# A second graph layer that reads stored transposed 0/1 rows instead of the adjacency matrix

## The chip, the cores and the metric

The kernel runs on one core of a Trainium2 chip. A core has four compute engines that each run their own instruction stream in order: PE (TensorE, matrix products; its weight loads are listed apart as PEld), DVE (VectorE), ACT (ScalarE) and POOL (GpSimd). SP (SyncE) issues most of the DMA transfers, POOL the indirect ones. Engines wait for each other through semaphores. The metric is the device time of one execution in microseconds (us), lower is better.

## What is computed

There are 16 batches of a graph with 1024 nodes and 64 features. `adj` is a symmetric 0/1 matrix with ones on its diagonal. Layer 0 removes some neighbours of every node ("dilation"), takes weighted quantiles of the features of those left, and runs a two-layer MLP. Layer 1 sums the features over the full adjacency and runs a second MLP. Both end in a residual and a layer norm.

```python
nb = (adj_ > 0) & (~eye)[None]                # neighbours without the node itself
m = nb.sum(-1)
rank = jnp.cumsum(nb, axis=-1) - 1
skip = jnp.where(m > 10, (m + 1) // 2, 1)
removed = nb & do_dil[..., None] & ((rank + 1) % skip[..., None] == 0)
rem = removed | jnp.swapaxes(removed, 1, 2)
...
# layer 0: agg = 0.25 q(0.25) + 0.5 q(0.5) + 0.25 q(0.75) over the neighbours left
x = _layernorm(x + (relu((x + agg) @ W1 + b1) @ W2 + b2) * mask)
# layer 1, on the full adjacency
messages = jnp.einsum('bij,bjh->bih', adjacency, h)
dh = jnp.tanh(jnp.concatenate([h, messages], -1) @ W1 + b1) @ W2 + b2
x = _layernorm(x + dh)
```

The edge updates of the second layer's reference don't reach its output and are not computed.

## The kernel before

A tile is 128 nodes, so a batch has eight tiles. The batches are taken in groups of 2, 4, 4, 4 and 2. Three kinds of work run for different groups at once.

**Lists** (`list_batch`, for the group that comes next). SP loads `adj` tile by tile into `a` (128x1024 f32, three buffers, L622) and `x` into the end of the row `nb` (L625). DVE clears the diagonal block (L623) and writes `nb` as 0/1 in bf16 (L626). ACT copies `nb` into `r`, only for the row sums that its accumulator gives (L630). PE transposes `nb` (L652), ACT copies that to `nb_t` (L654, two buffers), PE counts ranks with it in `p_rank` (L658, L660), ACT and DVE turn them into the removed edges (L662, L664). PE subtracts both directions of the removed edges in `p_val` (L672 to L675), ACT writes what is left back to `nb` (L677), and POOL scatters the rows to DRAM in order of degree (`order`, L712).

**Chunks** (`Chunk`, `ChunkByPE`, for the current group). `fetch_lists` loads rows of `order` (`row`, two buffers, L806), `fill` finds the neighbours in it and gathers their features, 1012 times on POOL (L846); the PE kind instead loads `row_p` (two buffers, L957), transposes it and selects by products with 0/1 matrices (`p_slots`, L990). `select` sorts with a network of minima and maxima on DVE (L875), forms the quantiles, runs the first MLP through the PSUM tiles `p_g`, `p_h` and `p_y` (L899 to L908; `p_y` has the single buffer of the tag "y"), and scatters the result to `x1` in DRAM (L916).

**Second layer** (`messages`, for the group before). Per batch, `x1` is loaded (L1018). Then, for each of the eight block rows (`QT` is 1), a row of `adj` is loaded again into `a` (L1024), PE transposes its eight blocks in f32 (`p_adj`, L1029), ACT copies them to `adj_t` (L1030), PE transposes `x1` (`p_x`, L1035) and sums the messages in f32 (`p_msg`, L1039), ACT copies both to `node_t` (L1036, L1041), and `p_z`, tanh and `p_d` follow (L1043 to L1048). DVE adds the bias to each block row (L1049). After the last one DVE adds `x1` (L1051), the layer norm runs, and SP stores the batch (L1053).

The loop at the end of the function (L1097 on) gives out steps of these generators in proportion to an estimate of each chunk's work (`Side`). A scheduler of the framework then orders the instructions of each engine; what the generators' order gives are priorities, not the final order. DMAs from SP and ACT share eight completion semaphores in turn, and a transfer waits until the one that last used its semaphore is complete. Pools give a tile's next user the buffer when the last reader is done. When the last group's chunks are over, the messages of its two batches run alone. `amiss` and `halves` hold tests of the data; if one fails, a general version of the whole computation follows (L1258), which does not run here.

Of the kernel before, what the change touches and what calls it, by code (L numbers as in the profile page):

```python
# [416 lines left out]
def kernel(  # L417
# [23 lines left out]
    QT = 1  # L441
# [13 lines left out]
    off_diag = const.tile([P, P], BF16, name="off_diag")  # L455
    nc.vector.tensor_scalar(off_diag, ident, -1.0, 1.0, op0=ALU.mult, op1=ALU.add)
# [4 lines left out]
    off_diag_f = const.tile([P, P], F32, name="off_diag_f")  # L461
    nc.vector.tensor_copy(off_diag_f, off_diag)
# [22 lines left out]
    zero = const.tile([P, BINS], F32, name="zero")  # L485
    nc.vector.memset(zero, 0.0)
# [30 lines left out]
    for i, (at, _, _) in enumerate(NETS[KTOP]["places"]):  # L517
        nc.gpsimd.memset(place_top[:, :, i], float(at))
    amiss = const.tile([P, B * NT], F32, name="amiss")
# [82 lines left out]
    class Group:  # L602
# [3 lines left out]
        def __init__(self, b0, count):  # L606
            self.b0, self.count, self.tiles, self.run = b0, count, count * NT, P // count
            self.order = [hbm.tile([N, ROW // 2], I32, name=f"order{b0 + i}") for i in range(count)]
            self.x1 = hbm.tile([count * N, C], F32, name=f"x1_{b0}")
            self.parts = []  # L610

    def list_batch(g, b):

        nbs, gone = [], []
        for half_b in range(2):
            at = slice(b * NT + half_b * HT, b * NT + (half_b + 1) * HT)

            m = rows.tile([P, 2, HT], F32, name="m")
            for t in range(half_b * HT, (half_b + 1) * HT):
                blk = slice(t * P, (t + 1) * P)  # L620
                a = rows.tile([P, N], F32, name="a", bufs=3)
                nc.sync.dma_start(a, adj[b, blk, :])  # L622
                nc.vector.tensor_mul(a[:, blk], a[:, blk], off_diag_f)  # L623
                nb = held.tile([P, ROW], BF16, name="nb")
                nc.sync.dma_start(nb[:, XCOL:].bitcast(F32), x[b, blk, :])  # L625
                nc.vector.tensor_scalar(nb[:, :N], a, 0.0, None, op0=ALU.is_gt)  # L626
# [12 lines left out]
            mh = halves[:, at]  # L639
            nc.vector.tensor_add(mh, m[:, 0], m[:, 1])  # L640
            nc.vector.tensor_scalar(mh, mh, 0.5, 0.25, op0=ALU.mult, op1=ALU.add)
            nc.vector.tensor_scalar(skip, mh, ROUND, -ROUND, op0=ALU.add, op1=ALU.add)
            nc.vector.scalar_tensor_tensor(do, mh, 0.5 * T_THRESH + 0.25, mask[:, at],
                                           op0=ALU.is_gt, op1=ALU.mult)
            nc.vector.scalar_tensor_tensor(want, skip, 1.0, do, op0=ALU.add, op1=ALU.mult)
            nc.vector.tensor_scalar(biases[0], skip, -3.0, -2.0 * FAR, op0=ALU.mult, op1=ALU.add)
            nc.vector.scalar_tensor_tensor(biases[1], m[:, 0], 2.0, biases[0], op0=ALU.mult, op1=ALU.add)
            for t in range(half_b * HT, (half_b + 1) * HT):
                nb, r, col = nbs[t], gone[t], slice(t - half_b * HT, t - half_b * HT + 1)
                p = ps_t.tile([P, N], BF16, name="p_nb", tag="tr")  # L650
                for j in range(NT):
                    nc.tensor.transpose(p[:, j * P:(j + 1) * P], nb[:, j * P:(j + 1) * P], ident_h)  # L652
                nb_t = rows.tile([P, N], BF16, name="nb_t")
                nc.scalar.copy(nb_t, p)  # L654

                for h in range(2):
                    p = ps_m.tile([P, HALF], F32, name="p_rank", tag="rv", bufs=3)
                    nc.tensor.matmul(p, far_h, nb[:, h * HALF:(h + 1) * HALF], start=True, stop=False)  # L658
                    for c in range(HT):
                        nc.tensor.matmul(p[:, c * P:], nb_t[:, (h * HT + c) * P:(h * HT + c + 1) * P],  # L660
                                         reach[:, :HALF - c * P], start=False, stop=c == HT - 1)
# [25 lines left out]
        nc.vector.tensor_scalar(low, deg, float(BINS - 1), None, op0=ALU.min)  # L687
# [8 lines left out]
        nc.vector.tensor_tensor_scan(base[:, 1:], zero, p[:, :BINS], 0.0, op0=ALU.add, op1=ALU.add)  # L696
# [89 lines left out]
    class Chunk:  # L786
# [12 lines left out]
        def fetch_lists(self):  # L799
# [3 lines left out]
            for t in range(self.t0, self.t0 + self.n):  # L803
                row = nets.tile([P, N], BF16, name="row")
# [57 lines left out]
        def select(self):  # L862
# [19 lines left out]
            for h in range(0, n, HT):  # L882
# [23 lines left out]
                p_y = ps_m.tile([P, HT, C], F32, name="p_y", tag="y", bufs=1)  # L906
# [15 lines left out]
    class ChunkByPE(Chunk):  # L922
# [13 lines left out]
        def fill(self):  # L936
# [8 lines left out]
            for q in range(g.count // 2):  # L945
# [9 lines left out]
                for i in range(2):  # L955
                    row = nets.tile([P, N], BF16, name="row_p")
# [57 lines left out]
    def messages(g, b):  # L1014

        x1 = work.tile([P, NT, C], F32, name="x1_n", bufs=1)
        n0 = (b - g.b0) * N
        nc.sync.dma_start(x1, g.x1[n0:n0 + N, :].rearrange("(t p) c -> p t c", p=P))  # L1018
        d = work.tile([P, NT, C], F32, name="d", bufs=1)
        for h in range(NT // QT):  # L1020
            adj_t = nets.tile([P, NT, QUART], F32, name="adj_t", bufs=1)
            for t in range(QT):
                a = rows.tile([P, N], F32, name="a", bufs=3)
                nc.sync.dma_start(a, adj[b, (h * QT + t) * P:(h * QT + t + 1) * P, :])  # L1024
                for q in range(2):
                    p = ps_t.tile([P, HT, P], F32, name="p_adj", tag="ta")
                    for j in range(HT):
                        col = (q * HT + j) * P
                        nc.tensor.transpose(p[:, j, :], a[:, col:col + P], ident)  # L1029
                    nc.scalar.copy(adj_t[:, q * HT:(q + 1) * HT, t * P:(t + 1) * P], p)  # L1030
                yield
# [6 lines left out]
            for j in range(NT):  # L1038
                nc.tensor.matmul(p[C:2 * C, :QUART], x1[:, j, :], adj_t[:, j, :],  # L1039
                                 start=(j == 0), stop=(j == NT - 1))  # L1040
# [5 lines left out]
            p_d = ps_m.tile([P, QT, C], F32, name="p_d", tag="y", bufs=1)  # L1046
            for t in range(QT):
                nc.tensor.matmul(p_d[:, t, :], z_t[:, t * P:(t + 1) * P], w2b_s, start=True, stop=True)  # L1048
            nc.vector.tensor_add(d[:, h * QT:(h + 1) * QT], p_d, b2b_r[:, None, :].to_broadcast([P, QT, C]))  # L1049
            yield  # L1050
        nc.vector.tensor_add(d, d, x1)  # L1051
# [45 lines left out]
    for s in range(-LEAD, len(plan)):  # L1097
# [48 lines left out]
    nc.vector.tensor_tensor(amiss, amiss, halves, op=ALU.max)  # L1146
    nc.vector.tensor_reduce(worst, amiss, AX.X, ALU.max)
# [14 lines left out]
    nc.vector.memset(ones_row, 1.0)  # L1162
    ps_t = ctx.enter_context(tc.tile_pool(name="ps_t_g", bufs=2, space=PSUM))
# [7 lines left out]
    def dilate(adj_b, mask_b):  # L1171
# [3 lines left out]
        for t in range(NT):  # L1175
            blk = slice(t * P, (t + 1) * P)
            a = rows.tile([P, N], F32, name="a")
# [173 lines left out]
```

## Time and profile before

| | us |
|---|---|
| median of three timed runs (3123.43 to 3137.13) | 3128.27 |
| span of the profiled execution | 3776.8 |
| PE busy in it | 2604.1 |
| DVE busy | 2394.6 |
| ACT busy | 1582.8 |
| POOL busy | 1522.6 |

The profiled execution is a fifth longer than the timed ones. A line of a group reads: line of the source, engine, operation, what is written and read, shapes and count, then busy time, mean ns of one, and the time that the engine stood idle just before these instructions with what ended most of it. A line of a wait reads: who waited, for whom, us in total, times, longest us. "issue" means that the trace shows nothing that was waited for. PEclk is the share of PE's full clock that was granted, 0.815 on average over this span.

### The profile page before, as it was taken

What the parts mean: (1) busy time and instruction counts of PE and PEld (TensorE: products, weight loads), DVE (VectorE), ACT (ScalarE), POOL (GpSimd) and SP (SyncE); (2) the same over time, 40 slices, a digit from 0 to 9 for tenths busy, and PEclk for the clock granted to TensorE, in tenths of its full rate; (3) what the DMA queues carried; (4) which work ended last, traced back from release to release, by engine and by line L of the source; (5) the groups of instructions that cost most, each with busy time, mean ns of one, the idle gap of its engine ahead of it and who ended that gap; (6) DMA issues with size and microseconds to landing.
All of it is one profiled execution on the core that took longest, in us unless ns stands there. A gap on an engine that the chain in (4) does not pass through costs nothing. (4 is left out here: it accounts for less than half of the span.)

```text
span 3776.8 us, 65923 instructions
## 1 busy us (share of the span) xinstructions
PE 2604.1 (69%) x25076; PEld 1957.5 (52%) x25076; DVE 2394.6 (63%) x5580; ACT 1582.8 (42%) x4045; POOL 1522.6 (40%) x1512
## 2 busy tenths in 40 slices
PE   5545767484875777756887598747879366677777
PEld 2424544262654555535765376525657255565565
DVE  4546774483867766846886467737879368675461
ACT  6523546452433435533554255413445133343353
POOL 3253262436335423652462524462552554423310
PEclk8866888696987887867988798768989677788898
DMA  3401133141312222131333122212222121121222
GB/s 122 132 20 57 52 88 122 46 117 32 95 44 76 80 69 65 43 102 43 93 95 98 41 82 75 68 35 72 78 75 54 39 76 55 39 68 47 61 68 77
DMA packets 221333, 264.34 MB, mean 70 GB/s; under 512 B 147443, under 2 KB 148050, under 8 KB 221008
## 3 DMA queue, kind: packets, MB, share of 16 engines
q1 hardware_dynamic: 174288, 189.31, 17.1%
q0 software_dynamic: 46720, 70.74, 7.0%
q8 instruction: 199, 3.26, 0.4%
q14 instruction: 126, 1.03, 0.1%
HBM read 218.20 MB, written 46.40 MB: 70 GB/s over the span
## 5 line engine op out<-in xcount | busy, mean ns | idle before, releaser
L846 POOL DMA_INDIRECT slots_a<-in_x_dram,idx x1012 | 1185.5, 1171 | 940.0 <-issue 290.2
L990 PE MATMUL p_slots<-hot,parts 128*64 128x256 bf16 (+1 forms) x12288 | 807.7, 275 | 296.6 <-issue 239.5
L990 PEld LDWEIGHTS <-parts 128*64 128x64 bf16 x12288 | 653.2, 115 | 444.3 <-issue 402.1
L982 DVE TENSOR_SCALAR hot<-val 128x2048 bf16<-128x2048 bf16 x456 | 307.3, 693 | 323.0 <-remote 279.9
L916 POOL DMA_INDIRECT x<-y,ids x128 | 165.7, 1295 | 826.4 <-DVE y L558 633.1
L875 DVE TENSOR_TENSOR slots_b<-slots_a 128x256 f32<-128x256 f32 (+14 forms) x582 | 356.4, 627 | 151.2 <-remote 58.6
L1001 ACT COPY slots_a<-p_slots 128x512 f32<-128x512 f32 (+2 forms) x136 | 73.3, 539 | 765.9 <-PE p_slots L990 326.1
L899 PE MATMUL p_g<-ident,terms 128*64 128x128 f32 x1988 | 299.0, 306 | 77.4 <-ACT terms L897 63.2
L1039 PE MATMUL p_msg<-adj_t,x_n 128*64 128x128 f32 x2048 | 288.4, 292 | 65.2 <-issue 53.6
L899 PEld LDWEIGHTS p_g<-ident,terms 128*64 128x64 f32 x1988 | 254.7, 155 | 118.0 <-ACT terms L897 89.8
L1039 PEld LDWEIGHTS p_msg<-adj_t,x_n 128*64 128x64 f32 x2048 | 241.2, 146 | 98.0 <-issue 73.8
L875 DVE TENSOR_TENSOR slots_a<-slots_b 128x256 f32<-128x256 f32 (+11 forms) x526 | 286.2, 556 | 0.6
L660 PE MATMUL p_rank<-reach,nb_t 128*128 128x512 bf16 (+3 forms) x1024 | 204.2, 337 | 90.0 <-ACT nb_t L654 59.6
L662 ACT ACTIVATE gone<-p_rank,s 128x512 bf16<-128x512 f32 x256 | 168.0, 685 | 123.5 <-PE p_rank L660 54.8
L1029 PE MATMUL p_adj<-ident,a 128*128 128x128 f32 x1024 | 191.3, 302 | 39.2 <-ACT adj_t L1030 13.4
L660 PEld LDWEIGHTS <-nb_t 128*128 128x128 bf16 x1024 | 99.8, 108 | 228.3 <-issue 89.0
L1049 DVE TENSOR_TENSOR d<-p_d,b2b_r 128x64 f32<-128x64 f32 x128 | 28.2, 221 | 285.0 <-PE p_d L1048 167.6
L825 DVE MAX8 key<-code 128x8 f16<-128x1024 f16 x170 | 207.4, 1220 | 2.0 <-DVE code L827 0.5
L630 ACT ACTIVATE gone<-nb 128x512 bf16<-128x512 bf16 x256 | 159.8, 627 | 114.2 <-DVE nb L626 96.0
L712 POOL DMA_INDIRECT order<-nb,at_i x128 | 147.7, 1154 | 147.8 <-DVE at_i L708 58.9
L875 DVE TENSOR_TENSOR slots_b<-slots_b 128x256 f32<-128x256 f32 (+11 forms) x310 | 197.7, 638 | 0.4
L677 ACT ACTIVATE nb<-p_val 128x512 bf16<-128x512 f32 x256 | 151.6, 596 | 90.0 <-remote 53.6
(189 smaller groups left out, 4682.3 us busy)
## 6 DMA issues: line engine op xcount, KB each, us to landing
a<-in_adj_dram SPq DMA_DIRECT2D x256, 512.0 KB
row_p<-order SPq DMA_DIRECT2D x64, 256.0 KB
slots_a<-in_x_dram,idx POOLq DMA_INDIRECT x1012
row<-order SPq DMA_DIRECT2D x192, 64.0 KB
nb<-in_x_dram SPq DMA_DIRECT2D x128, 32.0 KB
row<-order SPq DMA_DIRECT2D x32, 128.0 KB
x_s<-in_x_dram SPq DMA_DIRECT2D x16, 256.0 KB
x_n<-x SPq DMA_DIRECT2D x16, 256.0 KB
```

Source lines behind the costliest of these rows:

```text
L630: nc.scalar.activation(r[:, cols], nb[:, cols], AF.Copy, accum_out=m[:, h, t - half_b * HT:t - half_b * HT + 1])
L660: nc.tensor.matmul(p[:, c * P:], nb_t[:, (h * HT + c) * P:(h * HT + c + 1) * P], reach[:, :HALF - c * P], start=False, stop=c == HT - 1)
L662: nc.scalar.activation(r[:, h * HALF:(h + 1) * HALF], p, AF.Abs, bias=biases[h][:, col], scale=2.0)
L825: nc.vector.max(key[:, t, r:r + 8], code)
L846: nc.gpsimd.indirect_dma_start(out=self.a[:, at[k], t, :], out_offset=None, in_=x_rows, in_offset=bass.IndirectOffsetOnAxis(ap=idx[:, t, k ...
L875: nc.vector.tensor_tensor(view(rb, ra, [(d[0], d[1 + side]) for d in dims]), view(ab, aa, [(d[0], d[1]) for d in dims]), view(bb, ba, [(d[ ...
L899: nc.tensor.matmul(p[:C, col], terms[:, i], ident, start=False, stop=t == e - 1 and first + i == places - 1)
L916: nc.gpsimd.indirect_dma_start(out=g.x1, out_offset=bass.IndirectOffsetOnAxis(ap=g.local[:, self.t0 + t:self.t0 + t + 1], axis=0), in_=y[: ...
L982: nc.vector.tensor_scalar(hot[:, :, :, e], val, float(inside[at]), None, op0=ALU.is_equal)
L990: nc.tensor.matmul(p[i * C:(i + 1) * C, o:o + w], g.parts[2 * q + i][:, c, h], hot[:, c, i, :w], start=c == 0 and h == 0, stop=c == NT - 1 ...
L1029: nc.tensor.transpose(p[:, j, :], a[:, col:col + P], ident)
L1039: nc.tensor.matmul(p[C:2 * C, :QUART], x1[:, j, :], adj_t[:, j, :], start=(j == 0), stop=(j == NT - 1))
```

## The change

- List stage: DVE no longer clears the diagonal or makes `nb`. ACT copies `a` into `nb` in bf16, with the row sums from its accumulator, so `nb` now has the diagonal; 1 is subtracted from the half that holds it, and one more matmul each in `p_rank` and `p_val` takes it out. Beside it DVE compares `a` with itself and with zero and counts (`plain`), a test that all of `adj` is 0 or 1. The diagonal is loaded apart, one transfer of 1024 single elements per batch (`own_edge`), and tested at the end.
- `nb_t` is stored to DRAM by a DMA that ACT issues (`turned`, 256 KB per tile).
- Second layer: `QT` is 2, so there are four steps per batch. Each loads two stored tiles (`nbr_t`, one buffer, 512 KB); the transposes and copies of `adj` are gone. `x1` is split once per batch into three bf16 parts, and `p_msg` is 24 bf16 matmuls of 256 columns. `p_d` collects the whole batch in PSUM and is added once.
- Buffers: `row` and `row_p` have one instead of two; `p_y` moves from the tag "y" to the two buffers of "m", and `p_d` holds "y".
- Smaller: `low` is clipped and rounded, a scan's constant operand is `ones_h`, and some constants go or move.

```diff
-    QT = 1
+    QT = 2
...
+            self.turned = [hbm.tile([N, N], BF16, name=f"turned{b0 + i}") for i in range(count)]
...
+        nc.sync.dma_start(own_edge[:, b * NT:(b + 1) * NT], bass.AP(
+            tensor=adj.tensor, offset=adj[b].offset, ap=[[N + 1, P], [P * (N + 1), NT], [1, 1]]))
...
-                nc.vector.tensor_mul(a[:, blk], a[:, blk], off_diag_f)
...
-                nc.vector.tensor_scalar(nb[:, :N], a, 0.0, None, op0=ALU.is_gt)
...
-                    nc.scalar.activation(r[:, cols], nb[:, cols], AF.Copy,
+                    nc.scalar.activation(nb[:, cols], a[:, cols], AF.Copy,
                                          accum_out=m[:, h, t - half_b * HT:t - half_b * HT + 1])
+                nc.vector.scalar_tensor_tensor(r, a, 0.0, a, op0=ALU.is_gt, op1=ALU.is_equal,
+                                               accum_out=plain[:, b * NT + t:b * NT + t + 1])
...
+            nc.vector.tensor_scalar(m[:, half_b], m[:, half_b], -1.0, None, op0=ALU.add)
...
                 nc.scalar.copy(nb_t, p)
+                nc.scalar.dma_start(g.turned[b - g.b0][t * P:(t + 1) * P, :], nb_t)
...
+                    if h == half_b:
+                        c = t - half_b * HT
+                        nc.tensor.matmul(p[:, c * P:], minus_h, reach[:, :HALF - c * P],
+                                         start=False, stop=True)
...
+                if h == t // HT:
+                    nc.tensor.matmul(p[:, (t % HT) * P:(t % HT + 1) * P], minus_h, ident_h,
+                                     start=False, stop=False)
...
-                row = nets.tile([P, N], BF16, name="row")
+                row = nets.tile([P, N], BF16, name="row", bufs=1)
...
-                p_y = ps_m.tile([P, HT, C], F32, name="p_y", tag="y", bufs=1)
+                p_y = ps_m.tile([P, HT, C], F32, name="p_y", tag="m")
...
-                    row = nets.tile([P, N], BF16, name="row_p")
+                    row = nets.tile([P, N], BF16, name="row_p", bufs=1)
...
+        parts = nets.tile([P, NT, 3, C], BF16, name="parts_1", bufs=1)
+        rest = work.tile([P, NT, C], F32, name="x1_rest", tag="wide", bufs=1)
+        for i in range(3):
+            nc.scalar.copy(parts[:, :, i], x1 if i == 0 else rest)
+            if i < 2:
+                nc.vector.tensor_sub(rest, x1 if i == 0 else rest, parts[:, :, i])
         d = work.tile([P, NT, C], F32, name="d", bufs=1)
+        nc.vector.tensor_add(d, x1, b2b_r[:, None, :].to_broadcast([P, NT, C]))
+        p_d = ps_m.tile([P, NT, C], F32, name="p_d", tag="y", bufs=1)
+        yield
         for h in range(NT // QT):
-            adj_t = nets.tile([P, NT, QUART], F32, name="adj_t", bufs=1)
-            for t in range(QT):
-                a = rows.tile([P, N], F32, name="a", bufs=3)
-                nc.sync.dma_start(a, adj[b, (h * QT + t) * P:(h * QT + t + 1) * P, :])
...
-                        nc.tensor.transpose(p[:, j, :], a[:, col:col + P], ident)
-                    nc.scalar.copy(adj_t[:, q * HT:(q + 1) * HT, t * P:(t + 1) * P], p)
-                yield
+            nbr_t = nets.tile([P, QT, N], BF16, name="nbr_t", bufs=1)
+            nc.sync.dma_start(nbr_t, g.turned[b - g.b0][h * QUART:(h + 1) * QUART, :].rearrange(
+                "(t p) n -> p t n", p=P))
...
-                nc.tensor.matmul(p[C:2 * C, :QUART], x1[:, j, :], adj_t[:, j, :],
-                                 start=(j == 0), stop=(j == NT - 1))
+                for i in range(3):
+                    nc.tensor.matmul(p[C:2 * C, :QUART], parts[:, j, i], nbr_t[:, :, j * P:(j + 1) * P],
+                                     start=j == 0 and i == 0, stop=j == NT - 1 and i == 2)
...
-            nc.vector.tensor_add(d[:, h * QT:(h + 1) * QT], p_d, b2b_r[:, None, :].to_broadcast([P, QT, C]))
...
-        nc.vector.tensor_add(d, d, x1)
+        nc.vector.tensor_add(d, d, p_d)
...
-                going = Side(finish_group(groups[i - 1]), groups[i - 1].count * (NT + NT // QT + 1))
+                going = Side(finish_group(groups[i - 1]), groups[i - 1].count * (NT // QT + 2))
```

More of the change, by code (lines that the diff above doesn't have):

```diff
@@ L454 @@
     nc.vector.tensor_copy(ident_h, ident)
-    off_diag = const.tile([P, P], BF16, name="off_diag")
-    nc.vector.tensor_scalar(off_diag, ident, -1.0, 1.0, op0=ALU.mult, op1=ALU.add)
     upper = const.tile([P, P], F32, name="upper")
@@ L460 @@
                             pattern=[[1, P]], channel_multiplier=-1)
-    off_diag_f = const.tile([P, P], F32, name="off_diag_f")
-    nc.vector.tensor_copy(off_diag_f, off_diag)
     minus_h = const.tile([P, P], BF16, name="minus_h")
@@ L484 @@
     nc.vector.memset(eps, EPS)
-    zero = const.tile([P, BINS], F32, name="zero")
-    nc.vector.memset(zero, 0.0)
     number = const.tile([P, B * NT], F32, name="number")
@@ L518 @@
         nc.gpsimd.memset(place_top[:, :, i], float(at))
+    plain = const.tile([P, B * NT], F32, name="plain")
+    own_edge = const.tile([P, B * NT], F32, name="own_edge")
     amiss = const.tile([P, B * NT], F32, name="amiss")
@@ L619, in list_batch @@
             for t in range(half_b * HT, (half_b + 1) * HT):
-                blk = slice(t * P, (t + 1) * P)
                 a = rows.tile([P, N], F32, name="a", bufs=3)
-                nc.sync.dma_start(a, adj[b, blk, :])
-                nc.vector.tensor_mul(a[:, blk], a[:, blk], off_diag_f)
+                nc.sync.dma_start(a, adj[b, t * P:(t + 1) * P, :])
                 nb = held.tile([P, ROW], BF16, name="nb")
-                nc.sync.dma_start(nb[:, XCOL:].bitcast(F32), x[b, blk, :])
-                nc.vector.tensor_scalar(nb[:, :N], a, 0.0, None, op0=ALU.is_gt)
+                nc.sync.dma_start(nb[:, XCOL:].bitcast(F32), x[b, t * P:(t + 1) * P, :])
                 r = held.tile([P, N], BF16, name="gone", bufs=NT)
@@ L660, in list_batch @@
                         nc.tensor.matmul(p[:, c * P:], nb_t[:, (h * HT + c) * P:(h * HT + c + 1) * P],
-                                         reach[:, :HALF - c * P], start=False, stop=c == HT - 1)
+                                         reach[:, :HALF - c * P], start=False,
+                                         stop=h != half_b and c == HT - 1)
+                    if h == half_b:
+                        c = t - half_b * HT
+                        nc.tensor.matmul(p[:, c * P:], minus_h, reach[:, :HALF - c * P],
+                                         start=False, stop=True)
                     nc.scalar.activation(r[:, h * HALF:(h + 1) * HALF], p, AF.Abs,
@@ L686, in list_batch @@
         low = work.tile([P, NT], F32, name="low", bufs=1)
-        nc.vector.tensor_scalar(low, deg, float(BINS - 1), None, op0=ALU.min)
+        nc.vector.tensor_scalar(low, deg, float(BINS - 1), 0.0, op0=ALU.min, op1=ALU.max)
+        nc.vector.tensor_scalar(low, low, ROUND, -ROUND, op0=ALU.add, op1=ALU.add)
         own = work.tile([P, NT, BINS], BF16, name="own", bufs=1)
@@ L695, in list_batch @@
         nc.vector.memset(base[:, 0:1], 0.0)
-        nc.vector.tensor_tensor_scan(base[:, 1:], zero, p[:, :BINS], 0.0, op0=ALU.add, op1=ALU.add)
+        nc.vector.tensor_tensor_scan(base[:, 1:], ones_h[:, :BINS], p[:, :BINS], 0.0, op0=ALU.mult, op1=ALU.add)
         p = ps_m.tile([P, NT, BINS], F32, name="p_at", tag="m")
@@ L1018, in messages @@
         nc.sync.dma_start(x1, g.x1[n0:n0 + N, :].rearrange("(t p) c -> p t c", p=P))
+        parts = nets.tile([P, NT, 3, C], BF16, name="parts_1", bufs=1)
[4 more added lines that the diff above has]
+                nc.vector.tensor_sub(rest, x1 if i == 0 else rest, parts[:, :, i])
         d = work.tile([P, NT, C], F32, name="d", bufs=1)
+        nc.vector.tensor_add(d, x1, b2b_r[:, None, :].to_broadcast([P, NT, C]))
+        p_d = ps_m.tile([P, NT, C], F32, name="p_d", tag="y", bufs=1)
+        yield
         for h in range(NT // QT):
-            adj_t = nets.tile([P, NT, QUART], F32, name="adj_t", bufs=1)
-            for t in range(QT):
-                a = rows.tile([P, N], F32, name="a", bufs=3)
[L1024 to L1030, printed above, removed]
-                yield
+            nbr_t = nets.tile([P, QT, N], BF16, name="nbr_t", bufs=1)
+            nc.sync.dma_start(nbr_t, g.turned[b - g.b0][h * QUART:(h + 1) * QUART, :].rearrange(
+                "(t p) n -> p t n", p=P))
             node_t = work.tile([2 * C, QUART], F32, name="node_t", bufs=1)
@@ L1045, in messages @@
             nc.scalar.activation(z_t, p[:C, :QUART], AF.Tanh, bias=b1b_c)
-            p_d = ps_m.tile([P, QT, C], F32, name="p_d", tag="y", bufs=1)
             for t in range(QT):
-                nc.tensor.matmul(p_d[:, t, :], z_t[:, t * P:(t + 1) * P], w2b_s, start=True, stop=True)
-            nc.vector.tensor_add(d[:, h * QT:(h + 1) * QT], p_d, b2b_r[:, None, :].to_broadcast([P, QT, C]))
+                nc.tensor.matmul(p_d[:, h * QT + t, :], z_t[:, t * P:(t + 1) * P], w2b_s, start=True, stop=True)
             yield
-        nc.vector.tensor_add(d, d, x1)
+        nc.vector.tensor_add(d, d, p_d)
         layer_norm(work, d, d)
@@ L1146 @@
     nc.vector.tensor_tensor(amiss, amiss, halves, op=ALU.max)
+    nc.vector.tensor_scalar(plain, plain, -1.0, float(N), op0=ALU.mult, op1=ALU.add)
+    nc.vector.tensor_tensor(amiss, amiss, plain, op=ALU.max)
+    nc.vector.tensor_scalar(own_edge, own_edge, 1.0, None, op0=ALU.not_equal)
+    nc.vector.tensor_tensor(amiss, amiss, own_edge, op=ALU.max)
     nc.vector.tensor_reduce(worst, amiss, AX.X, ALU.max)
@@ L1162 @@
     nc.vector.memset(ones_row, 1.0)
+    off_diag = work.tile([P, P], BF16, name="off_diag")
+    nc.vector.tensor_scalar(off_diag, ident, -1.0, 1.0, op0=ALU.mult, op1=ALU.add)
     ps_t = ctx.enter_context(tc.tile_pool(name="ps_t_g", bufs=2, space=PSUM))
@@ L1176, in dilate @@
             blk = slice(t * P, (t + 1) * P)
-            a = rows.tile([P, N], F32, name="a")
+            a = rows.tile([P, N], F32, name="a", bufs=3)
             nc.sync.dma_start(a, adj_b[blk, :])
```

## The prediction

> **What bounds the kernel now.** I read the page's busy line first, then windows of 100 us, the waits, the groups by shape and the end of the timeline. The page's chain covers only the last 2 us and decides nothing. Busy line, then two windows (columns: PE, PEld, DVE, ACT, POOL busy; PEclk, DMA share, GB/s):
>
> ```profile
> PE 2604.1 (69%) x25076; PEld 1957.5 (52%) x25076; DVE 2394.6 (63%) x5580; ACT 1582.8 (42%) x4045; POOL 1522.6 (40%) x1512
> ...
> 1800.00:1900.00 100.00, 88.69 (x983) 71.90 (x983) 90.36 (x198) 51.12 (x120) 52.91 (x33) 0.95 0.34 97
> ...
> 2525.00:2550.00 25.00, 3.34 (x9) 1.63 (x9) 0.00 (x0) 0.00 (x0) 19.20 (x20) 0.50 0.13 26
> ```
>
> In the full windows PE and DVE are both near 90%: two bounds side by side, PE slightly ahead over the span. The 25 us window is something else: PE starts a matmul every 2.4 us, waits for nothing that the trace shows ("issue"), and all but POOL stand still. Waits (us in total, times, longest us):
>
> ```profile
> PE p_slots L990 <- issue: 239.5, 297, 2.5
> DVE d L1049 <- PE p_d L1048: 167.6, 62, 15.6
> SPq L1024 <- PE p_adj L1029: 673.6, 65, 79.1
> SPq L806 <- DVE code L823: 299.5, 28, 62.1
> ```
>
> PE's "issue" rows add to 495 us, its waits for ACT to 374, for DVE to 220. The three timed runs (3123 to 3137) are 648 us shorter than this profiled span of 3776.8, about what those stalls would give back. I infer that the timed runs hold the same work with fewer stalls, with PE 83% and DVE 77% busy. The sum below is in us of the profiled span and carried over as us, not as a percentage.
>
> The second layer is in these groups (busy, mean ns | idle before):
>
> ```profile
> L1039 PE MATMUL p_msg<-adj_t,x_n 128*64 128x128 f32 x2048 | 288.4, 292 | 65.2 <-issue 53.6 <-ACT adj_t L1030 6.6 <-ACT z_t L1045 2.8
> L1029 PE MATMUL p_adj<-ident,a 128*128 128x128 f32 x1024 | 191.3, 302 | 39.2 <-ACT adj_t L1030 13.4 <-ACT ln_st L556 9.1 <-DMA a<-in_adj_dram 6.1
> L1030 ACT COPY adj_t<-p_adj 128x512 f32<-128x512 f32 x256 | 149.4, 584 | 78.1 <-PE p_adj L1029 59.5 <-remote 7.2 <-issue 5.7
> L626 DVE TENSOR_SCALAR nb<-a 128x1024 bf16<-128x1024 f32 x128 | 88.3, 691 | 43.2 <-DMA order<-nb,at_i 42.6
> L1049 DVE TENSOR_TENSOR d<-p_d,b2b_r 128x64 f32<-128x64 f32 x128 | 28.2, 221 | 285.0 <-PE p_d L1048 167.6 <-remote 86.8 <-PE p_nth L968 20.4
> L875 DVE TENSOR_TENSOR slots_b<-slots_a 128x1024 f32<-128x1024 f32 x27 | 32.1, 1218 | 33.6 <-PE p_g L899 16.4 <-remote 14.3 <-ACT terms L897 1.7
> ```
>
> L1049 works 28 us, but DVE stands 285 us in front of it. At the end the layer runs alone; two successive block rows in the timeline:
>
> ```profile
> 3693.99 1.96 PE L1039 MATMUL p_msg<-adj_t,x_n 128*64 128x128 f32 x16
> ...
> 3698.37 1.96 PE L1039 MATMUL p_msg<-adj_t,x_n 128*64 128x128 f32 x16
> ```
>
> So one block row of 128 nodes costs PE 4.38 us with no gap, at full clock.
>
> **What the Trainium skill says.** "TensorE: Matmul & The Clock Gate", Back-to-back issue gap: a warm bf16 matmul of N columns follows the last after N/2.4 + 2.5 ns, 109 ns at 256. The trace agrees: three p_nth matmuls of 256 columns take 0.49 us, two 0.38, a step of 0.11. Same page, What's actually happening: an idle array falls to half clock; the stalled window above shows PEclk 0.50. "VectorE: DVE Perf Modes", The perf-mode tier table: in fp32 an operation on two tensors runs 1x, one on a tensor and a scalar 2x; the 128x1024 rows above show 1218 against 691 ns. "DMA: Bandwidth & Descriptors", Rules for kernel authors: a strided last dimension becomes one descriptor per element; no transfer of that size is in this trace.
>
> **The change, part by part.** *PE.* Removed: 128 block rows of 4.38, 561 us. Added: 64 pairs of block rows. Each has 24 bf16 matmuls (23 x 0.11 + 0.27 = 2.80), two transposes (0.40), p_z as L903 does it at 64x256 (0.70), four passes of p_d as L908 (0.66): 4.56, less some 0.2 of overlap, 4.4; 64 of them, 282. List stage: one rank matmul more per tile, a quarter of the four that take 0.72 us (0.18, 23 us for 128), and one p_val matmul of 128 columns (four take 0.39; step 0.06, 7 us): 30. Net -249; 35 of it (70 against 35) lies in the exposed end, 214 elsewhere.
>
> *DVE.* Removed: L623 35.9, L626 88.3, L1049 28.2, together 152. Added: 128 comparisons of a with itself. Not in the trace; from below the 0.69 of L626, from above 1.22 plus 0.2 for the accumulator (ACT's reads take 0.19). I take 1.22: 156 us. Also 32 subtractions at 0.69 and 16 additions at 0.69 (33), small operations (8). Net +45. Of the 285 us in front of L1049, 85 are at the end; some 200 us of blocked DVE queue go, since d now waits 16 times. I count that as support for the share below, not again.
>
> *ACT.* Removed: 149 (L1030), 66 of node copies, 46 of tanh: 261. Added: 64 times (two copies at 0.37, tanh 0.48), 78; 48 part copies at 0.61, 29; 128 stores to issue at SP's 0.33 to 0.43, 49. Net -105, off the bound: worth zero. The copy into nb now reads a; 512 f32 elements take 614 ns (L726), as the 627 of L630: zero.
>
> *DMA and SP.* 64 MB of adj reads become 32 MB written and 32 MB read, at a mean share of 0.24: zero. In the built streams all 16 own_edge loads stand at SP's head among the first a loads: 1024 runs of 4 bytes each, 0.4 us to issue, 6.4 in all. A load of 1024 runs of 256 bytes is used 2.87 us after issue (3679.72 to 3682.59). Bounds 0 and 16 x 1.6 = 25 us; ACT paces the head, so I take +8. Fewer loads hold SP (L1024's 673.6 us): a gain not counted.
>
> *Buffers.* row goes to one: the first max pass after the multiply takes 1.22 us, a chunk at least 3.6, and a 512 KB load 3.5 (a issued at 23.33, used at 26.83), so the reload hides. row_p goes to one: the second load starts after the transposes, 3.5 less 0.9 exposed, 32 times: 0 to 83, mostly beside other PE work; I take +10. p_y moves beside p_g and p_h: zero, PE orders them anyhow. nbr_t has one buffer: in the built PE stream hundreds of instructions lie between most pairs, which hides the load; at the end seven, so there it shows.
>
> *The end,* 99 us from the last scatter (3677.6). After: 2.1 to the x1 load, 2.9 load, 4.0 for the parts (three copies, two subtractions, handoffs), 2.8, then three times (3.5 + 2.8), 3.0 to p_d: 31.6 for the first batch after the 2.1; 28.7 for the second, whose load is early; 13.5 for norm and store (3763.3 to 3776.8). 76, so -23.
>
> **Sum.** Of 214 us outside the end I pass on half, 107, because DVE (2440 with the additions) is then the busiest engine. -107 - 23 + 8 + 10 = -112: 3016 us.
>
> **Rivals.** *PE alone is the bound.* For: 397 us of DVE's idle time wait for PE by name, 447 more for something remote in the same stalls. All 214 pass: 3128 - 214 - 23 + 18 = 2909. Against: DVE at 90% in the best windows. *DVE or the fills are the bound.* Only the end gains, half of DVE's 45 passes: 3128 - 23 + 18 + 22 = 3145 at worst, 3123 if the 22 hide. For: those windows; against: DVE's waits for PE. *Slower: ACT waits before its stores.* Each of 128 stores waits for nb_t and, in the built stream, mostly for an earlier transfer's completion, often one from SP. SP stands up to 79 us on one wait. Behind the store on ACT lie the copies of p_rank, p_val and p_slots, and PE waits for these. A mean wait w on the path costs 128 w; from w = 0.9 us the gain is gone. At 1.5, 192: 3208. Against: SP's long waits are mostly back-pressure that comes early. The change does what it says: no loads of adj remain in messages.
>
> **Chances.** Forecast 0.55 (share 0.25 to 0.8, head 0 to 25: 2944 to 3086). PE alone 0.15. DVE or fills 0.12: 0.05 faster, 0.05 within, 0.02 slower. ACT waits 0.18, all slower but 0.01 within. About 0.5%, 16 us, is what this measurement can tell. Faster 0.75, same 0.06, slower 0.19. Range: from below "PE alone", 2870, to above "DVE or fills", 3150, leaving 0.05 and 0.15 outside.
>
> **What would show it.** p_msg near 24 x 0.11 a pair; PE busy near 2355, DVE near 2440, ACT near 1480; L1049's 285 us of idle DVE gone and not back at L1062; the end near 76; no DMA wait of tens of us in the first 100. Wrong if waits of ACT before L655, or of PE for nbr_t, add to over 100 us, or if DVE's idle time stays at 1380 while PE's grows by all of the 249.

## The result and the profile after

Before took 3132.7 us (3123 to 3145), after 3170.5 us (3165 to 3175): 1.012 of before, interval 1.0075 to 1.0159. The forecast of 3016 was on the wrong side, and the result lies above the range.

One thing must be known to read what follows: a chip is at times in a condition in which before takes 3790 to 3880 us, with PE stalling in "issue", and at other times free of these stalls, with before at 3130. The profile of before that the prediction worked from has the stalls; its timed runs and the whole result do not. Below, "stalling" and "free" name the two conditions, and each ratio is to the kernel before, run beside it on the same chip in the same condition.

The page of after, busy line:

```profile
PE 2206.6 (70%) x23510; PEld 1752.6 (55%) x23668; DVE 2445.6 (77%) x5550; ACT 1410.0 (44%) x3617; POOL 1804.4 (57%) x1512
```

The span is 3173.1, as the timed runs. DVE came out as forecast (2440) and ACT near it (1480); PE's 2355 had been counted from a stalling profile, which the experiments below show to overstate PE. DVE is now the busiest engine by 239 us. Two windows of after (PE, PEld, DVE, ACT, POOL busy, PEclk, DMA share, GB/s):

```profile
1800.00:1900.00 100.00, 93.71 (x1191) 75.97 (x1201) 81.56 (x178) 50.16 (x121) 71.00 (x55) 0.98 0.24 64
900.00:1000.00 100.00, 81.06 (x840) 63.44 (x846) 95.99 (x172) 52.32 (x121) 86.12 (x36) 0.93 0.21 56
```

PE still tops the first window, but the second shows what none of the windows of 100 us in the stalling profile of before has (90% at most): DVE at 96%, with PE at 81. The groups that answer those of before (busy, mean ns | idle before):

```profile
L1052 PE MATMUL p_msg<-nbr_t,parts 128*64 128x256 bf16 x1536 | 206.6, 295 | 38.0 <-ACT parts L1033 17.4 <-DMA nbr_t<-turned 12.3 <-ACT node_t L1048 4.4
L626 ACT ACTIVATE nb<-a 128x512 bf16<-128x512 f32 x256 | 159.5, 625 | 221.9 <-DMA order<-nb,at_i 118.1 <-DMA a<-in_adj_dram 80.1 <-issue 13.9
L629 DVE SCALAR_TENSOR_TENSOR gone<-a 128x1024 bf16<-128x1024 f32 x128 | 154.8, 1216 | 81.9 <-DMA a<-in_adj_dram 55.8 <-PE p_val L684 26.0
L1062 DVE TENSOR_TENSOR d<-d,p_d 128x512 f32<-128x512 f32 x16 | 10.9, 681 | 33.1 <-PE p_d L1060 33.0
```

The messages cost PE 207 us, and the transposes of `adj` are gone; one check costs 1216 ns, as assumed. ACT's copy into `nb` takes 625 ns, as forecast, but ACT stands 222 us in front of it, 118 of them until the scatter of an old row has landed. The 285 us of idle DVE before L1049 are 33 before L1062. Waits of after (us, times, longest):

```profile
DVE d L1037 <- DMA x_n<-x: 73.5, 4, 26.1
DVE slots_b L885 <- DMA slots_a<-in_x_dram,idx: 50.6, 4, 26.2
DVE idx L841 <- DMA slots_a<-in_x_dram,idx: 46.0, 2, 28.4
DVE m L639 <- ACT nb L626: 45.2, 9, 19.2
ACT nb_t L654 <- DMA turned<-nb_t: 1.4, 2, 1.0
```

So the idle time in front of DVE got other names (x1's load, gathers, ACT's copy). My slower rival feared that ACT would stand before its stores. In the timeline of after a store begins 0.03 us after the copy into `nb_t` in the median and 0.48 us on average over the 128, below the 0.9 us at which the gain would be gone; ACT waits another 1.4 us for a store that still holds `nb_t` (the last line). One such copy and its store:

```profile
33.93 1.03 ACT L654 COPY nb_t<-p_nb 128x1024 bf16<-128x1024 bf16 x1
...
34.99 0.33 ACTq L655 DMA_DIRECT2D turned<-nb_t  x1
```

The end, three pairs of block rows in the timeline, and below them windows inside these three groups:

```profile
3104.83 4.45 PE L1052 MATMUL p_msg<-nbr_t,parts 128*64 128x256 bf16 x24 [0.78 <-DMA nbr_t<-turned]
3112.90 4.21 PE L1052 MATMUL p_msg<-nbr_t,parts 128*64 128x256 bf16 x24 [1.31 <-DMA nbr_t<-turned]
3120.92 2.78 PE L1052 MATMUL p_msg<-nbr_t,parts 128*64 128x256 bf16 x24 [1.50 <-DMA nbr_t<-turned]
```

```profile
3104.90:3109.20 4.30, 4.30 (x24) 3.49 (x23) 0.00 (x0) 0.00 (x0) 0.00 (x0) 0.60 0.00 0
3113.00:3117.10 4.10, 4.10 (x24) 3.34 (x23) 0.00 (x0) 0.00 (x0) 0.00 (x0) 0.65 0.01 4
3121.00:3123.60 2.60, 2.60 (x24) 2.43 (x23) 0.00 (x0) 0.00 (x0) 0.00 (x0) 1.00 0.27 61
```

A pair takes 2.78 us, the forecast's 2.80, in the last of these and 4.2 to 4.5 in the others, with about 3.6 us from one group to the next. The Trainium skill, "TensorE: Matmul & The Clock Gate", What's actually happening, lets the array's clock fall by half once PE has idled for a while. The trace agrees: the granted clock is 0.60 and 0.65 in the two slow groups and 1.00 in the fast one. The end is 85 us (last scatter at 3087.8, span 3173.1) where 99 became 76 in the forecast.

### The profile page after: what moved, and what is told of

It reads as the page before. It is cut to its first block, busy times and chain, and to the rows that moved or that the text cites. A ratio compares the mean times of both kernels' runs of the same rounds, so it can differ in the third digit from the quotient of the medians.

```text
span 3173.1 us, 62253 instructions
## 1 busy us (share of the span) xinstructions
PE 2206.6 (70%) x23510; PEld 1752.6 (55%) x23668; DVE 2445.6 (77%) x5550; ACT 1410.0 (44%) x3617; POOL 1804.4 (57%) x1512
## 5 line engine op out<-in xcount | busy, mean ns | idle before, releaser
L856 POOL DMA_INDIRECT slots_a<-in_x_dram,idx x1012 | 1453.3, 1436 | 710.0 <-issue 306.7
L1000 PE MATMUL p_slots<-hot,parts 128*64 128x256 bf16 (+1 forms) x12288 | 710.4, 274 | 169.6 <-DVE hot L992 140.0
L1000 PEld LDWEIGHTS <-parts 128*64 128x64 bf16 x12288 | 647.3, 116 | 212.7 <-issue 128.0
L926 POOL DMA_INDIRECT x<-y,ids x128 | 178.7, 1396 | 288.5 <-DVE y L554 162.9
L909 PE MATMUL p_g<-ident,terms 128*64 128x128 f32 x1988 | 284.6, 297 | 82.7 <-ACT terms L907 82.1
L626 ACT ACTIVATE nb<-a 128x512 bf16<-128x512 f32 x256 | 159.5, 625 | 221.9 <-DMA order<-nb,at_i 118.1
L1052 PE MATMUL p_msg<-nbr_t,parts 128*64 128x256 bf16 x1536 | 206.6, 295 | 38.0 <-ACT parts L1033 17.4
L661 PE MATMUL p_rank<-reach,nb_t 128*128 128x384 bf16 (+3 forms) x956 | 177.1, 315 | 71.9 <-ACT nb_t L654 64.7
L629 DVE SCALAR_TENSOR_TENSOR gone<-a 128x1024 bf16<-128x1024 f32 x128 | 154.8, 1216 | 81.9 <-DMA a<-in_adj_dram 55.8
L1052 PEld LDWEIGHTS <-parts 128*64 128x64 bf16 x1536 | 179.5, 119 | 59.2 <-issue 26.4
L907 ACT ACTIVATE terms<-p_chosen,w_rest 128x64 f32<-128x64 f32 x464 | 103.9, 332 | 165.0 <-PE p_chosen L1021 144.4
L686 ACT ACTIVATE nb<-p_val 128x512 bf16<-128x512 f32 x256 | 152.3, 599 | 39.6 <-PE p_val L684 38.4
```

The source lines that it names most:

```text
L626: nc.scalar.activation(nb[:, cols], a[:, cols], AF.Copy, accum_out=m[:, h, t - half_b * HT:t - half_b * HT + 1])
L629: nc.vector.scalar_tensor_tensor(r, a, 0.0, a, op0=ALU.is_gt, op1=ALU.is_equal, accum_out=plain[:, b * NT + t:b * NT + t + 1])
L856: nc.gpsimd.indirect_dma_start(out=self.a[:, at[k], t, :], out_offset=None, in_=x_rows, in_offset=bass.IndirectOffsetOnAxis(ap=idx[:, t, k ...
L909: nc.tensor.matmul(p[:C, col], terms[:, i], ident, start=False, stop=t == e - 1 and first + i == places - 1)
L926: nc.gpsimd.indirect_dma_start(out=g.x1, out_offset=bass.IndirectOffsetOnAxis(ap=g.local[:, self.t0 + t:self.t0 + t + 1], axis=0), in_=y[: ...
L1000: nc.tensor.matmul(p[i * C:(i + 1) * C, o:o + w], g.parts[2 * q + i][:, c, h], hot[:, c, i, :w], start=c == 0 and h == 0, stop=c == NT - 1 ...
```

## The experiments

The theories at the start: A, DVE sets the pace, so PE's relief passes little and DVE's additions count. B, PE sets it, and the gain is eaten by new waits for transfers.

**A fresh look at before.** No edit.

> The kernel before, unchanged, for a profile whose span is near the timed runs. Both theories: 3130 us. If the profiled span is again hundreds of us longer than the timed runs, the PE 'issue' stalls belong to the profile; if it is near 3130, PE's 'issue' waits should add to well under 50 us and PE, DVE and ACT busy sums stay at 2604, 2395 and 1583 within 3%.

The kernel took 3788 us and not 3130, beside 3791 (1.001, 0.997 to 1.005), and its twelve executions lie at 3766 to 3817, the profiled one at 3780. So here the stalls are in every execution and not in the profiled one alone; profiled executions without them follow below.

```profile
PE 2602.0 (69%) x25076; PEld 1965.7 (52%) x25076; DVE 2396.2 (63%) x5580; ACT 1583.3 (42%) x4045; POOL 1531.7 (41%) x1512
```

PE's longest row of waits in it:

```profile
PE p_slots L990 <- issue: 220.9, 280, 2.4
```

PE again stands for nothing that the trace names. DVE's busy sum serves below as that of before; there is no free profile of before.

**Less PE work in before.**

```diff
-            for j in range(NT):
+            for j in range(1):
                 nc.tensor.matmul(p[C:2 * C, :QUART], x1[:, j, :], adj_t[:, j, :],
-                                 start=(j == 0), stop=(j == NT - 1))
+                                 start=True, stop=True)
```

> The kernel before with 7 of the 8 p_msg matmuls of a block row left out, so each node gets the sum over one eighth of its neighbours: 7/8 of 288 = 252 us of PE go, the size of PE's relief by the change; loads, transposes and copies stay. At the end 16 x 1.75 = 28 us go in any case. A: 30 to 70 us less, 3060 to 3100. B (PE-bound): 28 plus most of 224, 2880 to 2950.

> The kernel before with 7 of 8 p_msg matmuls left out (a sum over one eighth of the neighbours), 252 us of PE less. On the stalling chip it gave 116 us. On a chip without stalls A expects 30 to 70 us (28 of it at the end), PE as the bound 200 or more.

Stalling: 3676 against 3791, 0.974 (0.964 to 0.983), 116 us. Free: 3099 against 3136, 0.990 (0.987 to 0.993), 37 us. The expectation counted 28 us in the end in any case. The traces show less. The window from the last scatter on, in before (stalling) and here (free):

```profile
3677.60:3776.80 99.20, 71.52 (x453) 54.32 (x453) 12.60 (x34) 35.60 (x86) 0.94 (x1) 0.84 0.25 76
3006.90:3099.40 92.50, 67.80 (x229) 38.79 (x229) 12.61 (x34) 36.96 (x86) 0.93 (x1) 0.50 0.27 81
```

The end is 7 us shorter (6 in the stalling run, 93.3), although PE has 28 us less to do in it: its granted clock is 0.50 in place of 0.84, and what is left takes longer (four transposes of `adj` 1.11 us, where they took 0.66). Before's end is known from stalling runs alone, but with SHARES 20, further down, the end is 83 us in both conditions. Why the clock stays at half here, with PE still busy for 73% of the window, is not shown. Of the other 224 us of PE, then, 110 pass with the stalls (49%; 26 to 58 by the interval) and 30 without (13%; 7 to 16). Busy lines of the stalling and the free run, and a window of the free one (columns as above):

```profile
PE 2441.0 (67%) x23284; PEld 1793.1 (49%) x23284; DVE 2393.6 (65%) x5580; ACT 1577.5 (43%) x4041; POOL 1565.3 (43%) x1512
PE 2267.7 (73%) x23284; PEld 1735.1 (56%) x23284; DVE 2389.7 (77%) x5580; ACT 1571.9 (51%) x4041; POOL 1717.0 (55%) x1512
```

```profile
1500.00:1600.00 100.00, 87.90 (x915) 69.77 (x909) 97.80 (x205) 56.74 (x145) 54.65 (x40) 0.91 0.35 95
```

The same matmuls keep PE busy for 2441 us with the stalls and 2268 without, and DVE for 2394 and 2390: the stalls inflate PE's sum and not DVE's. In the free run PE has lost the work, and DVE is at 98% in this window of the middle: PE has little to give there. B falls for the kernel before; A's 30 to 70 us holds.

**More DVE work in before.**

```diff
                 nc.vector.tensor_scalar(nb[:, :N], a, 0.0, None, op0=ALU.is_gt)
                 r = held.tile([P, N], BF16, name="gone", bufs=NT)
+                nc.vector.scalar_tensor_tensor(r, a, 0.0, a, op0=ALU.is_gt, op1=ALU.is_equal,
+                                               accum_out=amiss[:, b * NT + t:b * NT + t + 1])
```

> The kernel before with one scalar_tensor_tensor of 128x1024 f32 per tile added on DVE, 128 x 1.22 = 156 us, its result not used. A: DVE paces the kernel before too, 80 to 140 us more, 3210 to 3270. B (PE paces the kernel before): under 40 us more, up to 3170.

Stalling: 3843 against 3791, 1.015 (1.012 to 1.018). That is 52 us for 156, a third, between A and B. There is no free run of it.

**The kernel after again, and without its check.**

```diff
-                nc.vector.scalar_tensor_tensor(r, a, 0.0, a, op0=ALU.is_gt, op1=ALU.is_equal,
-                                               accum_out=plain[:, b * NT + t:b * NT + t + 1])
```

> The kernel after without L629, so the test that every entry of adj is 0 or 1 is left out: 128 x 1.22 = 155 us of DVE go, nothing else. Theory A (DVE sets the pace of the kernel after): 80 to 140 us less than after, 3030 to 3090, thus faster than before. Theory B (PE's and ACT's new waits on transfers set it): 0 to 30 less, 3140 to 3170.

> The kernel after, unchanged, beside the kernel before on one chip. If this chip runs without PE's 'issue' stalls (before near 3130): 1.012 of before, 3170. If it stalls as the chip of the first four runs did (before near 3790): by A (DVE's work sets the time) 1.00 to 1.02 of before; by B (the new waits) the stalls hide them, 0.96 to 0.99.

> The kernel after without L629 (the test of adj for 0 and 1 left out), against f1 on the same chip: 155 us of DVE go. A: 80 to 140 us less than f1. B: 0 to 30 less.

Stalling, without the check: 3813 against 3791, too scattered (3737 to 3823) for an interval. Free: after 3188 (1.018, 1.012 to 1.024), without the check 3222 (1.027, 1.023 to 1.032). Taking 155 us from the busiest engine gained nothing and seems to have cost 34; the two intervals just meet. Neither A nor B had that. The busy line of the kernel without the check (free), and one wait each of DVE and POOL:

```profile
PE 2232.9 (69%) x23668; PEld 1755.6 (55%) x23668; DVE 2305.6 (72%) x5295; ACT 1408.8 (44%) x3613; POOL 1693.0 (53%) x1512
```

```profile
DVE idx L840 <- DMA slots_a<-in_x_dram,idx: 182.1, 8, 32.3
...
POOL x L925 <- DVE y L555: 259.4, 10, 47.1
```

DVE's busy time fell by 138 us, and its wait in front of `idx` for old gathers rose from 46 us to 182. `idx` holds the row numbers by which POOL gathers. It has two buffers, so the third chunk's write must wait until the first one's gathers have landed. One such wait in the timeline, first POOL, then DVE:

```profile
2215.30 1.00 POOL L855 DMA_INDIRECT slots_a<-in_x_dram,idx  x1 [0.30 <-issue]
2216.60 1.00 POOL L855 DMA_INDIRECT slots_a<-in_x_dram,idx  x1 [0.30 <-issue]
2245.25 1.02 POOL L925 DMA_INDIRECT x<-y,ids  x1 [27.65 <-DVE y L555]
```

```profile
2218.93 0.21 DVE L840 TENSOR_TENSOR idx<-off,srt 128x48 int32<-128x48 f32 x1 [32.12 <-DMA slots_a<-in_x_dram,idx]
```

POOL gathers at one per 1.30 us while DVE stands 32 us in front of `idx`. Then POOL comes to a scatter of `y`, which DVE has not reached since it stood, and waits 28 us. Each in turn stands for the other. How much of the 34 us this makes is not shown here.

**The same instructions in another order.** Theory D: every edit makes the scheduler choose anew, and 1 to 2% is chance. C and R put the loss into the list half or the second layer.

```diff
-    SHARES = 24
+    SHARES = 20
```

> The kernel after with SHARES 20 in place of 24: the same instructions, given out in other portions, so ordered otherwise by the scheduler. D, the 1 to 2 per cent are chance of the order: over 20 us from the 3188 of after, either way. C and R: within 15 us.

> The kernel after with SHARES 20 in place of 24 (same instructions, another order), again, to have it on a chip that runs without PE's stalls (before near 3135). D, the order by chance decides 1 to 2 per cent: over 0.6 per cent from after's 1.012 to 1.018 of before, either way. C and R: 1.010 to 1.020 of before. On a stalling chip (before near 3800) it settles nothing new: 0.98 to 1.00.

Stalling 0.986 (0.976 to 0.996); free 3192, 1.018 (1.013 to 1.024), as after itself, though the instruction streams differ in thousands of places. D finds no support in this one reordering. In the free run DVE waits 78 us in front of `idx` (46 in after) although the kernel takes no longer than after, so such waits don't add to the span one for one. The free and stalling ratios lie on opposite sides of 1.

**The halves.** The list half has after's L612 to L686 without the stored rows, and before's second layer. The second-layer half has before's list stage with the store, after's `messages` and its buffers (one each for `row` and `row_p`, `p_y` under "m"), and

```diff
+                    if j == 1 and i == 0:
+                        for t in range(QT):
+                            for k in range(3):
+                                nc.tensor.matmul(p[C:2 * C, t * P:(t + 1) * P], parts[:, h * QT + t, k], ident_h,
+                                                 start=False, stop=False)
```

> The second layer of after (stored rows, bf16 parts, one add per batch) with the list stage of before; x1 itself is added by six small bf16 products with the identity, since the stored rows lack the diagonal. The first runs showed that neither PE's nor DVE's busy time alone sets the span, so the theories are now: C, the loss lies in the list half (the head, and ACT standing before its copy into nb until the scatter of the old row is done): this kernel 3060 to 3120 where before is 3136. R, the loss lies in the second layer (x1's load first used by DVE and ACT at the start of a batch, single row buffers): 3150 to 3190.

> The list stage of after (ACT makes nb, DVE checks adj, own_edge loads, the two extra products) without the stored rows, and the second layer of before with its loads of adj. C: 3160 to 3210 where before is 3136, with the first list batch's scatter about 10 us and the second's about 20 us later than in the kernel before. R: 3130 to 3150.

> The list stage of after without the stored rows, with the second layer of before, again, hoping for a chip without PE's stalls (before near 3135). On a stalling chip it was 1.0085 of before. C, the loss lies in the list half: 3160 to 3210. R, it lies in the second layer: 3130 to 3150. Its first two list batches: scattered at about 95 and 155 us by both, as on the stalling chip.

> The second layer of after with the list stage of before, again, on the same chip as the list half. On a stalling chip it was 0.9987 of before. C: 3060 to 3130, since PE is relieved and the end is shorter. R: 3150 to 3190.

> The list stage of after without the stored rows, with the second layer of before. On two stalling chips it was 1.008 of before, 32 us. On a chip without PE's stalls (before near 3135): C, the loss lies in the list half, 3160 to 3210; R, it lies in the second layer, 3130 to 3150.

> The second layer of after with the list stage of before, same chip. On two stalling chips 0.996 to 0.999 of before. On a chip without stalls: C, 3060 to 3130; R, 3150 to 3190.

> The second layer of after with the list stage of before, once more for a chip without PE's stalls. If before is near 3135: C (the list half carries the loss), 3060 to 3130; R (the second layer does), 3150 to 3190. On a stalling chip, as before, 0.995 to 0.999 of before.

| | stalling, three chips | free |
|---|---|---|
| list half | 1.0085, 1.0081, 1.0083 (1.004 to 1.013) | none |
| second layer | 0.9987, 0.9959, 0.9953 (0.991 to 1.001) | 1.0081 (1.0058 to 1.0103) |

Free, the second-layer half, with PE relieved and the end 16 us shorter than the 99 of before, costs 25 us by its ratio (its median, 3163, lies in R's 3150 to 3190). So the loss is not in the list half alone, and C's 3060 to 3130 falls. What remains to after's 1.012 to 1.018 would fall to the list half, but only by subtraction: it has no free run. Nor does this half part the new messages from the single row buffers. The busy line of the second-layer half (free; its profiled span, 3130.6, is at the low end of its 3130 to 3180):

```profile
PE 2220.2 (71%) x23796; PEld 1750.0 (56%) x23796; DVE 2403.1 (77%) x5515; ACT 1403.2 (45%) x3615; POOL 1727.0 (55%) x1512
```

and DVE's longest row of waits in it:

```profile
DVE idx L830 <- DMA slots_a<-in_x_dram,idx: 115.9, 5, 25.8
```

DVE's work is that of before; the wait for `idx`, 56 us in before with one message product, is 116. PE waits 52 us for `row_p`, 2 in before.

**A third idx buffer,** without the check, and without its tile `plain`:

```diff
-            idx = work.tile([P, 96], I32, name="idx")[:, :n * wide].rearrange("p (t k) -> p t k", k=wide)
+            idx = work.tile([P, 96], I32, name="idx", bufs=3)[:, :n * wide].rearrange("p (t k) -> p t k", k=wide)
```

> The kernel after without L629 (the test of adj left out) and with three idx buffers in place of two. With two, DVE stood 182 us before idx (8 times, until gathers of an earlier chunk had landed). If that wait is why 155 us less of DVE work did not pay: 3040 to 3100. If it was only where slack showed: 3190 to 3220.

> The kernel after without L629 (the test of adj for 0 and 1 left out) and with three idx buffers in place of two, once more for a chip without PE's stalls. There, with two buffers, it was 1.027 of before (3222), DVE stood 182 us before idx, and POOL stood 594 us for DVE: each waits for the other, through buffers. If the second idx buffer is what turned 155 us less of DVE work into a loss: 0.97 to 0.995 of before, 3040 to 3120. If DVE's slack would only show elsewhere: 1.015 to 1.03. On a stalling chip 0.992, as before.

Stalling 0.992 (0.989 to 0.995). Free: 3059 against 3130, 0.975 (0.968 to 0.983). Against 3222 with two buffers on another chip, this is 164 us for 384 bytes per partition. Busy line of the free run, and its waits before `idx` for gathers:

```profile
PE 2196.2 (72%) x23515; PEld 1743.4 (57%) x23668; DVE 2305.4 (75%) x5292; ACT 1409.4 (46%) x3615; POOL 1718.9 (56%) x1512
```

```profile
DVE idx L838 <- DMA slots_a<-in_x_dram,idx: 0.2, 1, 0.2
```

The busy sums are close to those of the run with two buffers. The wait of 182 us is gone, and DVE's idle time as a whole is 154 us shorter, so most of it did not come back elsewhere. This kernel is faster than before and, by the ratios, than after. But like before it has no check that `adj` is 0 or 1, and unlike before it relies on it, since its list stage and its messages read `adj` as a bf16 copy. Neither after with its check nor before was tried with a third buffer. Before with one message product waits 56 us in front of `idx` too, so part of the gain over before may be the buffer's and not the change's.

## Why the prediction was wrong

The free profiles, as DVE's busy time and the rest of the span:

| free run | span | DVE busy | DVE idle |
|---|---|---|---|
| before, one message product | 3099 | 2390 | 710 |
| second-layer half | 3131 | 2403 | 728 |
| after | 3183 | 2443 | 739 |
| after, SHARES 20 | 3196 | 2443 | 754 |
| after, no check, two idx buffers | 3219 | 2306 | 913 |
| after, no check, three | 3064 | 2305 | 759 |

But for the row with the idx waits, DVE's idle time stays at 710 to 759; before's, from its 3136 and 2396, is 740. The pattern is coarse: its spread of 49 us is larger than the loss of 38. PE is named as what ended only 135 to 210 us of the idle time; the rest are mostly handoffs from ACT and waits for transfers, and they remain when PE gets faster.

- *The step that failed* is the sum's "Of 214 us outside the end I pass on half". In the free run with one message product 13% passed (30 of 224 us), and the second-layer half, with PE's whole relief, was 25 us slower than before. The rest of PE's relief became waiting: in after PE waits 140 us for DVE's `hot`, and for rows and for ACT. The half was not wrong of the profile it was read from: there 49% passed. It was wrong to carry it, as I said I would, "as us of the profiled span" to timed runs 648 us shorter in which PE's stalls, the very thing that made PE scarce, are absent. I put PE at 83% of the timed runs, from a busy sum that the stalls inflate.
- *DVE's +45* was right (2443 less 2396 is 47), but the sum put it at nothing: it served only as a reason for the share, and the rival took half of it. From after to the best kernel 138 us less of DVE go with 129 us less of time (3188 to 3059). If the third buffer does no more than remove after's own 46 us of waiting for `idx`, 60 to 93% of that DVE work counts. This is argued; adding 156 us under stalls cost a third, and taking the check away with two buffers gained nothing.
- *Head.* +8 was too small. In free runs the last scatter of the second list batch starts at 134.8 us in before with one message product, at 143.4 in the second-layer half (the stores alone), at 148.5 in after without the check, at 157.0 in after: +22, of it some 9 for the stores and 8 for the check. I count it whole into the span, since all later work stands behind it; that is argued. What `own_edge` alone costs was not tried, and the 1.6 us a load behind my upper bound stand in no trace.
- *End.* -23 was -14. A pair's products do take 2.78 us at full clock (forecast 2.80), but five of the eight groups ran at 0.50 to 0.65 of it and took 4.2 to 4.9.
- *Waits.* L1049's 285 us went and did not come back at L1062, but other waits took their place. In the free run of before with one message product L1049 has 147 of them, so part may have come with the stalls. PE's waits for `nbr_t` (12 us) and ACT's before its stores (62 at most in all) are small: the slower rival's mechanism did not occur at the size it needed. `row_p` with one buffer makes PE wait 64 us (2 in before); whether that lengthens the span was not tried, but the best kernel has 53 of it.
- *The rivals.* "PE alone is the bound" is refuted by the 13%. "DVE or the fills are the bound" comes nearest; its 3145 "at worst" was low in two terms. With them measured: 3133 - 14 (end) + 22 (head) + 47 (DVE) - 8 (the check's part of the head, counted twice) = 3180, between the two measured 3170 and 3188. That fit is partly luck. The sum leaves out the 13% of PE's 214 us, 28 us, and with them it gives 3152. For the second-layer half the same terms, again without PE's share, give 3131 - 16 (end) + 9 (head) + 7 (DVE) = 3131, where its median is 3163. So at least 18 to 36 us stay open; the single row buffers and the longer waits for `idx` in the second-layer half (116 us) are candidates that no run parts.

## What to carry to other kernels

Before a profile's waits are turned into a gain, its span must agree with the timed runs; where it does not, ask which engine the difference makes look scarce. When several engines stand at 70 to 80% and are tied through rings of few buffers, relief of one may not pass on, because a ring closes on it: look for the small tile that is written early by one engine and freed late by another's transfers. In the kernel without the check a third buffer of 384 bytes per partition gave 164 us; taking 252 us of matrix products from before gave 37.

## What the runs showed of the hardware

- The stalling condition: medians of 3791 to 3877 us for a kernel that else takes 3130 to 3136, with 495 and 404 us of PE waiting for nothing that the trace shows in the two profiles of before, in gaps of up to 2.5 us at `p_slots`. Chip 3 showed it at one time and not at another. Its cause stays open.
- Signs change with it: the second-layer half is 0.1 to 0.5% faster than before in that condition and 0.8% slower without.
- Less work for PE can mean a slower PE: with 7 of 8 message products left out, the end ran at a granted clock of 0.50 in place of 0.84 and was 7 us shorter, not 28.
- A gather on POOL takes longer in free runs (1.30 to 1.44 us on average, beside 1.13 to 1.24), at the same number of gathers. Why is not shown.
- The accumulator of a scalar_tensor_tensor adds a separate DVE instruction of 79 ns, 10 us for 128:

```profile
L629 DVE DVE_READ_ACCUMULATOR gone<-a 128x1 f32 x128 | 10.1, 79 | 0.0
```
